# Layer 2 of a two-layer graph attention kernel reads the one-hot matrices that layer 1 stored; own lookups by quarters of a node tile; unnormalised weights with three more product columns

## Chip, cores and metric

The kernel runs on one core of one Trainium2 chip. The metric is the device time of one launch in microseconds (us), here the median of three runs. All times below are in us unless marked ns.

## The reference, cut to what matters

There are 3125 nodes with 768 features and 53125 edges sorted by their destination (50000 drawn ones and one loop per node). Each layer is a graph attention: it multiplies the features by a weight matrix, gives each edge a logit from its source and its destination, turns the logits into weights by a softmax over each destination's edges, and adds up the weighted source rows. A second loop per node is added inside, so a node's own row counts twice. Layer 1 has 4 heads of 256 columns, layer 2 one head of 768.

```python
def gat_conv(x, edge_index, W, a_src, a_dst, bias, heads, out_ch, concat):
    ei = _add_self_loops(edge_index, n); src, dst = (ei[0], ei[1])
    xl = (x @ W).reshape(n, heads, out_ch)
    e = leaky_relu(alpha_src[src] + alpha_dst[dst], 0.2)   # alpha: xl with a_src, a_dst
    m = segment_max(e, dst); e = exp(e - m[dst])
    alpha = e / (segment_sum(e, dst)[dst] + 1e-16)
    return segment_sum(xl[src] * alpha, dst) + bias
h = relu(layer_norm(x))
h1 = relu(layer_norm(gat_conv(h, W1...))) + (h @ Wr1 + br1)
h2 = layer_norm(gat_conv(h1, W2...)) + (h1 @ Wr2 + br2)
return x + h2
```

## The kernel before, in words

The nodes are cut into `NB` = 25 tiles of 128 (the last has 53). The edges of a node tile, without the loops, are laid into `S` = 2176 slots, which are `J` = 17 slot tiles of 128. Since the edges are sorted by destination, slot tile j holds only destinations of one or two of the node tile's four quarters of 32 nodes; the list `QUARTERS` (line 31) says which. For each slot three lists lie in HBM: the destination within the node tile (`rel16_d`), the source (`src16_d`) and the source modulo 128 (`slo16_d`). A flag computed on the chip sends inputs that do not fit to another function (`any_order`), which does not run here.

**Lookups.** The kernel has to bring logit parts to each slot: that of the slot's source (one of 3125 nodes) and those of its destination. It does this with products on TensorE. `spread` (line 444) loads a list of a node tile broadcast to all 128 partitions, `one_hot` (449) compares it with the partition number, which gives a 128 x 2176 matrix in bf16 with one 1 per slot. `own_products` (457) multiplies each of its 17 column blocks with the destination tile's logit parts, each split into three bf16 terms (`parts_of`, 434). `source_values` (467) multiplies the one-hot of the source modulo 128 with the logit parts of all 25 source tiles and picks the right one with a second one-hot, `ohh` (built at 469), in the operations `pick` and a reduction. Layer 1 does the own lookups beside its dense products (`own_lookups`, 843) and the source lookups afterwards (the loop at 954). Layer 2 does both in `softmax` (568) and builds all the one-hots once more.

**Softmax.** `weights` (488) brings the slots' logits into rows (25 per head, one per node tile, 2176 long) by transposes, takes the segment maximum with two scans and a maximum, goes back by transposes, and forms the exponentials. It then does the same way there and back once more for the segment sums, takes the reciprocal (555) and scales the weights `al`. For layer 2 it also scales the loop's weight (`alo2`).

**Sums.** `sums` (600) goes over the node tiles. For each of the up to 17 slot tiles GpSimd issues an indirect DMA (677) that gathers 128 source rows of the table (3 KB each in layer 2) into one of 26 buffers `g`. VectorE makes `w` (645 in layer 2), a 128 x 32 or 128 x 64 matrix with the slot's weight in the column of its destination. TensorE multiplies `w` by the gathered rows (697), with the slot tiles in six `ROUNDS` that mix quarters. In layer 2 `last_of` (654) makes a second such matrix `wl`, which carries the loop's weight at the last slot of each destination, and a one-column product with ones (702) brings it to the node (`aw`, 628). `finish` adds the node's own row, and `end2` (1134) the bias, the norm, the residual and the store. After each round a step of the residual `h1 @ Wr2` runs on TensorE (`residual`, 1083; 8 steps of 4 matmul instructions a node tile and a bias product).

**What sets the order.** TensorE, VectorE and ScalarE run the sums in the order of the program text; in layer 2's lookups and softmax only TensorE does, and a list scheduler orders the rest. Each engine and each DMA queue (SyncE's for loads and most stores, GpSimd's for gathers) runs in its order. The residuals of the first `FIRST` = 9 node tiles are filled in between lookups and softmax steps (`fill`), the other 16 run in the sums. The gathers of layer 2 are released by `mark` (594), a copy that waits for the lookups of the second-last node tile, and each waits until the memory of its buffer is free.

Of the kernel before, what the change touches and what calls it, by code (L numbers as in the profile page):

```python
# [9 lines left out]
F32 = mybir.dt.float32  # L10
# [14 lines left out]
SLOPE = 0.2  # L25
# [7 lines left out]
CODE = 4096  # L33

# [27 lines left out]
def in_order(  # L62
# [55 lines left out]
    rel16_d = dram.tile([NB * S], I16, name="rel16_d")  # L118
# [3 lines left out]

    parts_d = dram.tile([2, C2], F32, name="parts_d")
# [22 lines left out]
    rell_s = const.tile([128, NB * J], F32, name="rell_s")  # L146
    alone = const.tile([128, NB], F32, name="alone")
    ones_c = const.tile([128, 1], F32, name="ones_c")
    nc.vector.memset(ones_c, 1.0)
# [70 lines left out]
    def edge_list(ep, pe):  # L220
# [11 lines left out]
        nc.sync.dma_start(pk_d[E:].rearrange("(p f) -> p f", p=128), pad)  # L232
        yield
# [46 lines left out]
    def windows(pe):  # L280

        W = L + P
        with tc.tile_pool(name="cw", bufs=1, side="right", reuse_waits="tile") as ep:
# [38 lines left out]
            for i, d in enumerate((rel16_d, src16_d, slo16_d)):  # L322
                nc.sync.dma_start(d.rearrange("(p f) -> p f", f=L), r16[:, i])

        with tc.tile_pool(name="wn", bufs=1, side="right", reuse_waits="tile") as ep:
            k16 = ep.tile([NB, S], I16, name="k16")
            nc.sync.dma_start(k16, rel16_d.rearrange("(b f) -> b f", f=S))
# [4 lines left out]
            for t, to in ((k16, rel_s), (s16, idx_s), (k16, rell_s)):  # L332
                tf = ep.tile([NB, S], F32, tag="tf", name="tf")
                if to is rell_s:
                    nc.vector.memset(tf[:, S - 1:], 0.0)
                    nc.vector.tensor_tensor(tf[:, :S - 1], k16[:, :S - 1], k16[:, 1:], OP.is_equal)
                    nc.vector.scalar_tensor_tensor(tf, tf, float(CODE), k16, op0=OP.mult, op1=OP.add)
                else:
                    nc.vector.tensor_copy(tf, t)
# [104 lines left out]
    def spread(pool, b, list_d, name, bufs=2):  # L444
        t = pool.tile([128, S], I16, name=name, bufs=bufs)
        nc.sync.dma_start(t, list_d[b * S:(b + 1) * S][None, :].to_broadcast([128, S]))
        return t

    def one_hot(pool, b, list_d, name, t=None):

        if t is None:
            t = spread(pool, b, list_d, name)
        oh = pool.tile([128, S], BF16, name="oh" + name, bufs=2)
        nc.vector.tensor_scalar(oh, t, node_f, None, op0=OP.is_equal)  # L454
        return oh

    def own_products(heads, pp, oh, tabd_b):

        pd = pp.tile([128, J, 3, 2 * heads], F32, name="pd", bufs=1)
        for j in range(J):  # L460
            nc.tensor.matmul(pd[:, j], oh[:P, j * 128:(j + 1) * 128], tabd_b, start=True, stop=True)  # L461
        return pd

    def own_values(own, b, pd):
        nc.vector.tensor_reduce(own[:, :, :, b], pd.rearrange("p j t v -> p j v t"), axis=AX.X, op=OP.add)

    def source_values(heads, al, b, pp, nq, G, oh, tabs, ohh, pick):

        nc.vector.tensor_tensor(
            ohh, iota_f[:, None, :NB].to_broadcast([128, J, NB]),  # L470
            hi_s[:, b * J:(b + 1) * J, None].to_broadcast([128, J, NB]), OP.is_equal)
# [16 lines left out]
    def weights(heads, own, al, alo_d, sr, rows, pp, nq, fill, steps):  # L488
# [69 lines left out]
        if heads == 1:  # L558
            nc.vector.tensor_mul(alo_d, eo, s)
            return  # L560
# [7 lines left out]
    def softmax(heads, asad, al, alo_d, pp, nq, fill, side, steps=(4, 10, 3, 13, 5)):  # L568


        V = 2 * heads
        with tc.tile_pool(name="so", bufs=1, side=side, reuse_waits="tile") as so:
            own = so.tile([128, J, V, NB], F32, name="own")
            with tc.tile_pool(name="sb", bufs=2, side=side, reuse_waits="tile") as sb:

                part = parts_of(sb, asad.rearrange("p b v -> p (b v)"), NB * V, "part")
# [6 lines left out]
                for b in range(NB):  # L583
# [6 lines left out]
                    for _ in range((steps[0] + b % 2) // 2 if b > 1 else 0):  # L590
                        next(fill, None)
# [1025 lines left out]
```

## Time and profile before

| | us |
|---|---|
| three runs | 2020.69, 2017.33, 2020.15; median 2020.15 |
| the profiled execution's own time | 2020.3 |
| its span, first to last instruction | 2018.6 |
| busy in the span: PE | 1885.2 (93%) |
| DVE | 1249.0 (62%) |
| POOL | 877.6 (43%) |
| ACT | 277.2 (14%) |

The engines are PE (TensorE's matmuls; PEld are its weight loads, which overlap them), DVE (VectorE), ACT (ScalarE), POOL (GpSimd) and SP (SyncE). A busy PE is not PE at its peak, since matmuls are pipelined and their ends are modelled. In rows of groups the columns are: line, engine, operation, out<-in with sizes, count, busy time, mean ns of one, then the idle time of the engine just before them and what ended it. In rows of a timeline: start, length, engine, line, operation, count, and in brackets the idle time before it. In the chain of waits, which is followed back from the last instruction: start, length, what. The names of tiles carry no buffer numbers. A matmul in float32 shows as two instructions.

### The profile page before, as it was taken

The numbers are of one execution on the slowest core, as the hardware profiler recorded it, in microseconds if no ns is written. First come the engines' busy times: TensorE is split into PE (matmuls) and PEld (weight loads), VectorE is DVE, ScalarE is ACT, GpSimd is POOL, SyncE is SP. The second block draws the span as 40 slices with busy tenths as digits, with TensorE's granted clock in tenths as the row PEclk, the third lists the DMA queues.
The fourth block names the chain that finished last, engine by engine and source line by source line (L and its number), as shares of the span: only waits on it lengthen the run. The fifth ranks groups of instructions, "written<-read, shape, count | busy, mean of one in ns | idle before, by whom it ended". The sixth has DMA issues, their size and how long they took to land.

```text
span 2018.6 us, 38267 instructions
## 1 busy us (share of the span) xinstructions
PE 1885.2 (93%) x15033; PEld 1021.5 (51%) x15033; DVE 1249.0 (62%) x3352; ACT 277.2 (14%) x611; POOL 877.6 (43%) x911
## 2 busy tenths in 40 slices
PE   6999998999969999999999999789999999898986
PEld 4666665665424444544455554467544344343432
DVE  7774346888843555555456665468856655665665
ACT  1221463001201111112111111100100000000000
POOL 2200000000056656665666664000077777777774
PEclk9999999999989999999999999889999999998998
DMA  5531564331399999999999998588399999999996
GB/s 197 171 103 69 197 240 173 121 124 61 131 355 417 404 369 396 403 387 375 395 392 409 411 399 320 173 313 306 121 350 369 376 363 379 358 362 350 350 339 244
DMA packets 177687, 593.93 MB, mean 294 GB/s; under 512 B 32973, under 2 KB 45936, under 8 KB 177116
## 3 DMA queue, kind: packets, MB, share of 16 engines
q0 software_dynamic: 95840, 385.22, 50.0%
q1 hardware_dynamic: 78130, 196.57, 27.1%
q10 hardware_dynamic: 3530, 9.60, 1.2%
q8 instruction: 122, 2.00, 0.4%
q14 instruction: 65, 0.53, 0.1%
HBM read 528.32 MB, written 62.99 MB: 293 GB/s over the span
## 4 chain that ended last, share of the span: by engine, by line
PE 70%; DMA 14%; DVE 9%; POOL 3%; issue 2%; ACT 1%; SPq 0%; POOLq 0%; DVEq 0%; ACTq 0%
PE pa L697 18%; PE p L1052 13%; PE pm L800 13%; DMA g<-table,idx_s 11%; PE pr L1090 7%; PE pm L934 7%; PE pr L1002 4%; PE pq L478 4%; POOL g L677 3%; PE p L1030 1%; DMA s<-slo_d 1%; PE pd L461 1%; ACT h1T L1035 1%; PE pt L777 1%; DVE w L645 1%
## 5 line engine op out<-in xcount | busy, mean ns | idle before, releaser
L677 POOL DMA_INDIRECT g<-table,idx_s x832 | 827.4, 994 | 848.2 <-ACT rt L722 439.6
L697 PE MATMUL pa<-g,w 128*32 128x256 f32 (+1 forms) x6744 | 610.6, 426 | 75.2 <-DMA g<-table,idx_s 47.8
L697 PEld LDWEIGHTS pa<-g,w 128*32 128x32 f32 x6744 | 229.1, 110 | 417.9 <-issue 158.9
L1090 PE MATMUL pr<-wr,h 128*128 128x384 f32 (+1 forms) x800 | 299.3, 511 | 4.2 <-DMA h<-h1T_d 4.2
L1052 PE MATMUL p<-w,h1T 128*128 128x384 f32 (+2 forms) x800 | 278.2, 495 | 2.2 <-DVE h1T L1037 1.5
L800 PE MATMUL pm<-w,h 128*128 128x344 f32 (+1 forms) x900 | 271.9, 458 | 2.6 <-ACT h L779 2.6
L800 PEld LDWEIGHTS pm<-w,h 128*128 128x128 f32 (+1 forms) x900 | 166.7, 189 | 87.3 <-issue 6.9
L1052 PEld LDWEIGHTS p<-w,h1T 128*128 128x128 f32 (+1 forms) x800 | 143.8, 187 | 121.4 <-issue 34.1
L1090 PEld LDWEIGHTS pr<-wr,h 128*128 128x128 f32 (+1 forms) x800 | 142.2, 191 | 81.2 <-issue 13.8
L934 PE MATMUL pm<-h,wr 128*128 128x512 f32 x384 | 174.9, 607 | 0.0
L650 DVE TENSOR_TENSOR w<-oh,al 128x128 f32<-128x128 f32 (+1 forms) x416 | 141.6, 340 | 32.5 <-PE pa L697 12.3
L645 DVE TENSOR_SCALAR w<-iota_f,rel_s,al 128x32 f32<-128x32 f32 (+1 forms) x416 | 132.4, 325 | 44.7 <-PE pa L702 43.0
L659 DVE TENSOR_SCALAR wl<-iota_f,rell_s,alo 128x32 f32<-128x32 f32 (+1 forms) x416 | 134.9, 326 | 7.2 <-PE pa L702 6.7
L427 ACT ACTIVATE bn_sd<-bn_mv,eps 128x1 f32<-128x1 f32 (+1 forms) x50 | 14.7, 294 | 775.9 <-DVE bn_mv L423 729.7
L478 PEld LDWEIGHTS <-ohs 128*128 128x128 bf16 x2550 | 95.5, 97 | 35.8 <-issue 19.3
L934 PEld LDWEIGHTS pm<-h,wr 128*128 128x128 f32 x384 | 72.0, 194 | 79.5 <-issue 79.1
L1037 DVE TENSOR_TENSOR h1T<-h1T,r1t 128x512 f32<-128x512 f32 (+1 forms) x50 | 34.0, 680 | 125.9 <-ACT h1T L1035 120.6
L478 PE MATMUL pq<-tabs,ohs 128*128 128x100 bf16 (+1 forms) x2550 | 98.2, 191 | 11.3 <-DVE ohs L454 8.0
L649 DVE TENSOR_SCALAR oh<-iota_f,rel_s 128x32 f32<-128x32 f32 (+1 forms) x416 | 105.0, 252 | 4.8 <-DMA alo_d<-own 4.8
L1002 PE MATMUL pr<-h0k,wr 128*128 128x512 f32 (+1 forms) x288 | 106.8, 490 | 0.0
L1059 DVE COPY asad<-p 128x2 f32<-128x2 f32 (+1 forms) x25 | 4.0, 158 | 157.7 <-ACT row L1057 157.7
L702 PEld LDWEIGHTS pa<-ones_c,wl 128*32 128x32 f32 x1124 | 55.5, 112 | 56.9 <-issue 50.2
(222 smaller groups left out, 1493.0 us busy)
## 6 DMA issues: line engine op xcount, KB each, us to landing
d<-rel_d SPq DMA_DIRECT2D x50, 544.0 KB
s<-slo_d SPq DMA_DIRECT2D x50, 544.0 KB
g<-table,idx_s POOLq DMA_INDIRECT x832
table<-row SPq DMA_DIRECT2D x24, 512.0 KB
r1T_d<-rt SPq DMA_DIRECT2D x96, 128.0 KB
own<-table SPq DMA_DIRECT2D x24, 512.0 KB
r1t<-r1T_d SPq DMA_DIRECT2D x24, 512.0 KB
h1T_d<-h1T SPq DMA_DIRECT2D x24, 512.0 KB
```

The costliest lines, as they stand in the source:

```text
L478: nc.tensor.matmul(q[:, j], oh[:P, (j0 + j) * 128:(j0 + j + 1) * 128], tabs[:, i], start=(i == 0), stop=(i == 2))
L645: nc.vector.tensor_scalar(w[:, 0, :], iota_f[:, lo:hi], rel_s[:, c:c + 1], al[:, j, 0, b:b + 1], op0=OP.is_equal, op1=OP.mult)
L649: nc.vector.tensor_scalar(oh, iota_f[:, lo:hi], rel_s[:, c:c + 1], None, op0=OP.is_equal)
L650: nc.vector.tensor_tensor(w, oh[:, None, :].to_broadcast([128, heads, hi - lo]), al[:, j, :, b:b + 1].to_broadcast([128, heads, hi - lo]), ...
L659: nc.vector.tensor_scalar(w, iota_f[:, lo:hi], rell_s[:, c:c + 1], alo_d[:, j, 0, b:b + 1], op0=OP.is_equal, op1=OP.mult)
L677: nc.gpsimd.indirect_dma_start(out=g, out_offset=None, in_=table[:, :], in_offset=bass.IndirectOffsetOnAxis(ap=idx_s[:, b * J + j:b * J + ...
L697: nc.tensor.matmul(pa[32 * q:32 * q + 32, o // f, o % f:o % f + n], w[:, o // cols, :], g[:, o:o + n], start=to not in opened, stop=False, ...
L800: nc.tensor.matmul(pm[:r, :C], h0[gi][:, k, o:o + r], w1[:, k, i * C:(i + 1) * C], start=(k == 0), stop=(k == NK1 - 1))
L934: nc.tensor.matmul(pm[:, :GB * P], wr1[:, k, m * 128:(m + 1) * 128], h0[gi][:, k, :], start=(k == 0), stop=(k == NK1 - 1))
L1002: nc.tensor.matmul(pm[:, :nb], wr1[:, k, m * 128:(m + 1) * 128], loaded[gi, k][:, :nb], start=(k == 0), stop=(k == NK1 - 1))
L1052: nc.tensor.matmul(pm[:, :n], hT[:, k, :r], w2[:, k, o:o + n], start=(k == 0), stop=(k == NK2 - 1))
L1090: nc.tensor.matmul(pm[:, :384], h1[:, k, :r], wr2[:, k, i * 384:(i + 1) * 384], start=(k == 0), stop=False)
```

## The change

1. Layer 1 stores each node tile's one-hot matrices in HBM (`hot_d`, 128 x 3369 bf16 a node tile): the own one, the source one, and `ohh`, which is now bf16. The stores are issued on GpSimd's queue. Layer 2 loads them with one DMA a node tile into four buffers and builds none; `softmax` is gone.
2. Own lookups by quarters: partition group q (32 nodes) only sees slots 512q - 128 to 512q + 640 (`WIN` = 768, read from `rel16_d` with 128 entries in front). The one-hot has 768 columns instead of 2176; the table is spread over four column groups, of which each node fills its own quarter's (`by_quarter`); 6 products of 4 x 6 x heads columns take the place of 17 of 6 x heads.
3. Layer 2's weights stay unnormalised: `shares` does only the maximum's half of the softmax. Each `w` is multiplied with three columns `ends2` (1, whether the slot holds the maximum's weight or more, and that times twice the loop's weight), so the sum of the weights and the loop's weight come out in three PSUM columns beside the sums. `finish` makes the loop's weight `aw` and the factor `share` from them with six small operations, and `end2` scales. `wl`, `last_of`, `rell_s` and `alone` are gone.
4. `FIRST` is 3 instead of 9, and layer 2's residual steps run one a node tile from node tile 10 on in the lookups; the loads of `wr2` are spread over the lookups. With it there are 7 instead of 13 `xr` buffers.

```diff
+WIN = 768
+    hot_d = dram.tile([NB, 128, S + WIN + J * NB], BF16, name="hot_d")
...
-            for t, to in ((k16, rel_s), (s16, idx_s), (k16, rell_s)):
+            for t, to in ((k16, rel_s), (s16, idx_s)):
...
+    def window(pool, b):
+        t = pool.tile([128, WIN], I16, name="near", bufs=3)
+        for q in range(4):
+            o = b * S + 512 * q
+            nc.sync.dma_start(t[32 * q:32 * q + 32], rel16_d[o:o + WIN][None, :].to_broadcast([32, WIN]))
+        return t
+    def by_quarter(t, v, n, heads):
+        for i in range(3):
+            nc.vector.tensor_tensor(t[:, :, :, i, :], v(i)[:, :, None, :].to_broadcast([P, n, 4, 2 * heads]),
+                                    mine[:, None, :, None].to_broadcast([P, n, 4, 2 * heads]), OP.mult)
+    def own_products(heads, pp, oh, tabd_b, bufs=1):
+        pd = pp.tile([128, 512], F32, name="pd", bufs=bufs)[:, :20 * 6 * heads]
+        at = pd.rearrange("p (g r v) -> p r g v", r=4, v=6 * heads)
+        for c in range(WIN // 128):
+            nc.tensor.matmul(at[:, c % 4, c // 4:c // 4 + 4], oh[:, c * 128:(c + 1) * 128],
+                             tabd_b.rearrange("p q t v -> p (q t v)"), start=(c == 0), stop=True,
+                             skip_group_check=True)
...
+    def shares(al, own, share, ends, sr, pp, fill, steps):
...
+        nc.vector.tensor_tensor_scan(fw, pen[:, 0:S], xs, 0.0, op0=OP.add, op1=OP.max)
+        nc.vector.tensor_tensor_scan(bw[:, ::-1], pen[:, 1:S + 1][:, ::-1], xs[:, ::-1], 0.0, op0=OP.add, op1=OP.max)
+        nc.vector.tensor_max(fw, fw, bw)
...
+        nc.vector.tensor_sub(al, al, m)
+        nc.scalar.activation(share, al, AF.Exp)
+        nc.vector.tensor_sub(eo, eo, m)
+        nc.scalar.activation(eo, eo, AF.Exp)
+        nc.vector.tensor_scalar(ends[:, :, :, 1], al, -1.0, None, op0=OP.is_ge)
+        nc.vector.scalar_tensor_tensor(ends[:, :, :, 2], eo, 2.0, ends[:, :, :, 1], op0=OP.mult, op1=OP.mult)
...
             if heads == 1:
-                nc.vector.tensor_max(aw[:r], pa[:r, 1, f:f + 1], alone[:r, b:b + 1])
+                at = pa[:r, 1, f:f + 3]
+                v = gp.tile([P, 4], F32, name="v", bufs=2)[:r]
+                nc.vector.tensor_scalar(v[:, 0:1], at[:, 1:2], 0.1, 2.0, op0=OP.is_lt, op1=OP.mult)
+                nc.vector.tensor_scalar(v[:, 1:2], at[:, 1:2], 0.1, None, op0=OP.max)
+                nc.vector.reciprocal(v[:, 1:2], v[:, 1:2])
+                nc.vector.scalar_tensor_tensor(v[:, 2:3], at[:, 2:3], v[:, 1:2], v[:, 0:1], op0=OP.mult, op1=OP.add)
+                nc.vector.tensor_scalar(v[:, 3:4], at[:, 0:1], v[:, 2:3], 1e-16, op0=OP.add, op1=OP.add)
+                nc.vector.reciprocal(v[:, 3:4], v[:, 3:4])
+                aw, share = v[:, 2:3], v[:, 3:4]
...
-                        wl = last_of(b, j) if heads == 1 else None
...
-                    for q, wl in ends:
-                        nc.tensor.matmul(pa[32 * q:32 * q + 32, 1, f:f + 1], wl, ones_c, start=False, stop=False,
+                    for q, w, v in ends:
+                        nc.tensor.matmul(pa[32 * q:32 * q + 32, 1, f:f + 3], w, v, start=False, stop=False,
...
-                                ohs[b] = one_hot(sb, b, rel16_d, "d", ds_.pop(b))
+                                ohs[b] = one_hot(sb, ds_.pop(b), WIN, "ohd")
+                                nc.gpsimd.dma_start(hot_d[b, :, S:S + WIN], ohs[b])
...
+                        ohs = one_hot(sb, t, S, "ohs")
+                        nc.gpsimd.dma_start(hot_d[b, :, :S], ohs)
+                        ohh = sb.tile([128, J, NB], BF16, name="ohh", bufs=3)
...
+                        nc.gpsimd.dma_start(hot_d[b, :, S + WIN:], ohh.rearrange("p j b -> p (j b)"))
+                        source_values(H, al1, b, pp, 4, group_of(H), ohs, tabs, ohh, pick)
...
-        FIRST = 9
+        FIRST = 3
...
+                    for b in range(NB):
+                        hot = sb.tile([128, S + WIN + J * NB], BF16, name="hot", bufs=4)
+                        nc.sync.dma_start(hot, hot_d[b])
+                        pick = sb.tile([128, J, 1, NB], F32, name="pick")
+                        source_values(1, al, b, pp, 3, J, hot, tabs,
+                                      hot[:, S + WIN:].rearrange("p (j b) -> p j b", b=NB), pick)
+                        own_values(own, b, own_products(1, pp, hot[:, S:S + WIN], tabd[:, b]))
+                        if 1 <= b <= NK2:
+                            nc.sync.dma_start(wr2[:, b - 1, :], Wr2[(b - 1) * 128:b * 128, :])
+                        if b == 5:
+                            load(0)
+                        if b > NK2 + 1:
+                            next(fill)
+                        if b == NB - 2:
+                            behind = nc.gpsimd.tensor_copy(mark, al[:, 0, 0, b:b + 1]).ins
+                with tc.tile_pool(name="sr2", bufs=1, side="right", reuse_waits="tile") as sr:
+                    shares(al[:, :, 0, :], own, al2[:, :, 0, :], ends2, sr, pp, fill, (8, 4))
...
-            def end2(b, z):
-                nc.vector.tensor_add(z, z, b2_b[:z.shape[0]])
+            def end2(b, z, share):
+                nc.vector.scalar_tensor_tensor(z, z, share, b2_b[:z.shape[0]], op0=OP.mult, op1=OP.add)
```

More of the change, by code (lines that the diff above doesn't have):

```diff
@@ L232, in edge_list @@
         nc.sync.dma_start(pk_d[E:].rearrange("(p f) -> p f", p=128), pad)
+        none = ep.tile([1, P], I16, name="none")
+        nc.vector.memset(none, P)
+        nc.sync.dma_start(rel16_d[:P], none)
         yield
@@ L636, in finish @@
                                                pa[:r, o // f, o % f:o % f + n], op0=OP.mult, op1=OP.add)
-            yield from end(b, z)
+            yield from end(b, z, share)
         def weights_of(b, j):
@@ L1143, in in_order @@
             with tc.issue_after(behind):
-                sums(1, C2, table2, al2, alo2, 26, 1, gp, pp, end2, more, [each] * len(ROUNDS))
+                sums(1, C2, table2, al2, ends2, 26, 1, gp, pp, end2, more, [each] * len(ROUNDS))
 @with_exitstack
```

171 lines of the change are left out of this document (80 added, 91 removed).

## The prediction

> **What bounds the kernel now.** I read three views in this order: the page's span, the busy time by stage, and the timeline of GpSimd (POOL) in the second layer. The stages are layer 1's source lookups (350 to 485 us), layer 2's lookups (1288 to 1420), its softmax (1420 to 1461) and its sums (1461 to the end). Columns: stretch, busy time of PE, weight loads, DVE, ACT and POOL with instruction counts, granted clock, DMA share, GB/s.
>
> ```profile
> span 2018.6 us, 38267 instructions
> ```
>
> ```profile
> core 0: us, PE busy (x) PEld busy (x) DVE busy (x) ACT busy (x) POOL busy (x), PEclk, DMA share, GB/s
> 350.00:485.00 135.00, 133.15 (x1313) 85.98 (x1311) 114.61 (x151) 11.00 (x16) 0.00 (x0) 1.00 0.32 108
> 1288.00:1420.00 132.00, 116.56 (x1905) 81.24 (x1904) 92.61 (x220) 0.97 (x2) 1.65 (x2) 0.92 0.86 304
> 1420.00:1461.00 41.00, 38.74 (x168) 23.46 (x167) 34.82 (x28) 7.94 (x14) 0.00 (x0) 1.00 0.24 80
> 1461.00:2019.00 558.00, 494.26 (x3950) 222.15 (x3948) 342.97 (x1122) 7.36 (x25) 411.62 (x415) 0.97 0.95 349
> ```
>
> In the sums PE looks like the bound (494 of 558 us) and DMA too (0.95). The timeline of POOL says otherwise:
>
> ```profile
> 1414.45 0.67 POOL L594 COPY mark<-al 128x1 f32<-128x1 f32 x1 [171.53 <-DMA xr<-in_x_dram]
> 1415.50 0.98 POOL L677 DMA_INDIRECT g<-table,idx_s  x1 [0.38 <-DMA xr<-in_x_dram]
> 1461.29 1.16 POOL L677 DMA_INDIRECT g<-table,idx_s  x1 [44.81 <-DVE s L551]
> 1462.75 0.95 POOL L677 DMA_INDIRECT g<-table,idx_s  x1 [0.30 <-issue]
> ...
> 1999.64 0.95 POOL L677 DMA_INDIRECT g<-table,idx_s  x1 [0.30 <-issue]
> ...
> 2013.11 0.95 ACTq L172 DMA_DIRECT2D out_dram<-z  x2
> ```
>
> The first gather goes out at 1415.5; the second waits 44.8 us for DVE, because its buffer lies on memory that the softmax still uses (line 551). From 1461.3 to 2000.6 the other 415 gathers follow without a break, one every 1.300 us (539.3 / 415), and 18.0 us after the last one the span ends. The groups of the sums confirm it:
>
> ```profile
> L677 POOL DMA_INDIRECT g<-table,idx_s x393 | 390.2, 993 | 121.3 <-issue 75.9 <-DMA g<-table,idx_s 23.8 <-PE pa L702 13.7
> L697 PE MATMUL pa<-g,w 128*32 128x384 f32 x2168 | 281.5, 503 | 50.9 <-DMA g<-table,idx_s 35.0 <-DVE w L645 6.0 <-DVE wl L659 5.4
> L1090 PE MATMUL pr<-wr,h 128*128 128x384 f32 x457 | 174.8, 512 | 0.0
> L659 DVE TENSOR_SCALAR wl<-iota_f,rell_s,alo 128x32 f32<-128x32 f32 x250 | 79.0, 317 | 6.8 <-PE pa L702 6.3 <-PE pa L697 0.5
> L702 PE MATMUL pa<-ones_c,wl 128*32 128x1 f32 x1084 | 46.2, 170 | 0.0
> ```
>
> POOL's idle time is 121.3 / 393 = 0.31 us ahead of each gather, the constant gap between two issues: it never waits for a buffer, while PE waits for gathers (35.0 us) and DVE. So the end is **the start of the gather run, plus 539 us, plus 18 us**, and an edit pays if it moves that start, or the layer 1 before it.
>
> **The change, part by part.**
>
> *Layer 2's lookups.* The timeline has the end of their last reduction, the chain of waits their start (1298.9, when the last node tile's logits exist; that stays) and one tile:
>
> ```profile
> 1418.18 0.59 DVE L483 TENSOR_REDUCE al<-pick 128x17 f32<-128x425 f32 x1
> ```
>
> ```profile
> 1298.92 0.20 DVE part L438
> ...
> 1346.16 1.27 PE pq L478 x51
> 1347.44 0.42 PE pd L461 x17
> 1347.86 2.69 PE pr L1090 x8
> ```
>
> Now a tile costs PE 1.27 + 0.42 + 2.69 = 4.38 us, the last being two residual steps. After, the 17 own products become 6 (6 x 0.025 = 0.15), there is no residual step up to tile 9, and one (1.34) from tile 10: 1.42, then 2.76 us a tile. DVE loses both one-hots and `ohh`:
>
> ```profile
> L454 DVE TENSOR_SCALAR ohs<-s,node_f 128x2176 bf16<-128x2176 int16 x25 | 19.5, 779 | 10.2 <-DMA s<-slo_d 10.2
> L469 DVE TENSOR_TENSOR ohh<-iota_f,hi_s 128x425 f32<-128x425 f32 x25 | 14.8, 595 | 0.5 <-PE p L1030 0.5
> ```
>
> Of its 92.6 us in this stage 2 x 19.5 + 14.8 go; the 39 left bound nothing. What bounds it is DMA. A tile now loads 128 x 3369 x 2 B = 0.862 MB instead of two broadcasts of 0.557 MB. In the changed program four of these loads stand ahead of the last `table2` store on SP's queue, the rest behind it, so they flow from 1299: 21 x 0.862 + `wr2` 3.15 + four `h1` 2.10 + four `xr` 1.57 = 24.9 MB. At what rate?
>
> ```profile
> DMA packets 12175, 40.08 MB, mean 304 GB/s; under 512 B 2296, under 2 KB 2296, under 8 KB 12157
> ```
>
> ```profile
> 1500.00:1550.00 50.00, 44.79 (x352) 19.98 (x348) 32.09 (x112) 0.59 (x2) 38.42 (x39) 1.00 1.00 382
> ```
>
> The stage before, with its waits, had 304; a full stretch of gathers 382. Rows of 6.7 KB that stand queued are nearer to the second; I take 370: 67 us, to 1366. PE's own bound is close: tile 10 lands after 10.1 MB, at 1326, and 15 x 2.76 us later it is 1368. With the last picks and reductions the lookups end at **1372**, instead of at 1418.8. Bounds: 1368 (PE) and 1385 (304 GB/s). SP's new waits (for a free `hot` buffer, and one `h1` load that waits for a residual on PE with five `hot` loads behind it) have three loads in flight to cover them.
>
> The Trainium skill, DMA: Bandwidth & Descriptors, section Specifications, gives 358 GB/s as HBM's limit for a core; by it the lookups would end 2 us later. The row with 382 disagrees.
>
> *Start of the gathers.* The gather buffers now lie lower (fewer `xr` and no `wl` buffers): only the second and third touch softmax memory, the tile `keep`, whose last reader is the instruction that makes `pen`. In the changed program this stands on DVE behind the last reduction and four small operations, and ahead of the scans. So the run starts at 1372 + 4 = **1376**, 85 us earlier. But now it runs beside the scans:
>
> ```profile
> 1424.05 4.68 DVE rows L530
> 1428.72 4.59 DVE bw L531
> 1433.34 2.41 DVE rows L533
> ```
>
> ```profile
> 1715.04 0.95 POOL L677 DMA_INDIRECT g<-table,idx_s  x1 [0.31 <-PE pa L702]
> ...
> 1716.22 0.96 DVE L1135 TENSOR_TENSOR z<-z,b_b 128x768 f32<-128x768 f32 x1
> 1716.29 1.71 POOL L677 DMA_INDIRECT g<-table,idx_s  x1 [0.30 <-issue]
> ```
>
> A gather issued just after DVE began an operation on two SBUF tensors took 1.71 instead of 0.95 us: it ended about when it could if it had waited for DVE's end. Scans and maximum (11.7 us) are such operations, and some five of 0.6 us besides. If one gather slips through at each boundary, the run loses some **8 us**; bounds 0 and 14.7. The gain is 85 - 8 = 77 us.
>
> The Trainium skill, SBUF — State Buffer, section Who interferes with whom, has it that DVE with two SBUF inputs and GpSimd share a port under an exclusive lock, held for a whole instruction. The two rows agree; taken strictly it is the 14.7 us, 7 more than my sum, and it speaks against this overlap.
>
> *The softmax* loses its second pass of scans, sums, transposes and the reciprocal; it is not what the gathers wait for any more. Weights `w` exist some 26 us after 1372 (transposes, the scans and maximum above, exponentials, two residual additions): at about 1399. With 26 buffers and a gather each 1.3 us POOL doesn't run out by then (23 / 1.3 = 18).
>
> *The sums.* `wl` goes (391 operations of DVE, by the row of its narrower form 317 ns each), six small operations a node tile come; DVE had slack. The three-column products take the place of the one-column ones, as many. The cost is in `FIRST` = 3: six more residuals, 22 instead of 16, run here. A round of PE when nothing is late:
>
> ```profile
> 1834.48 1.56 PE L1090 MATMUL pr<-wr,h 128*128 128x384 f32 x4
> 1835.97 1.50 PE L697 MATMUL pa<-g,w 128*32 128x384 f32 x16
> 1837.28 0.22 PE L702 MATMUL pa<-ones_c,wl 128*32 128x1 f32 x8
> 1837.43 1.56 PE L1090 MATMUL pr<-wr,h 128*128 128x384 f32 x4
> ```
>
> One residual step takes 1.49 us, the round's products 1.46. After, 176 steps fall on 141 rounds: 1.46 + 1.25 x 1.49 + 0.09 for the biases = 3.41 us for 2.77 gathers, 1.23 us a gather against POOL's 1.30. From 1399 PE needs 415 x 1.23 = 510 us, to 1909; the last gather is issued at 1376 + 8 + 539 = 1923. PE stays hidden, with some 14 us to spare. DMA carries 5.5 MB more, about 10 GB/s, on top of the 349, below the 382 seen. The last tile's end gains five small operations: **+1 us**.
>
> *Layer 1.* Its PE is full, so PE's work counts:
>
> ```profile
> 300.74 0.41 PE pd L461 x17
> ...
> 337.88 2.30 PE pq L478 x51
> ```
>
> ```profile
> L343 PE MATMUL pe<-ident,tf x51: 214/215/238, 148.1 to 185.0; 25*128 25x25 f32 x51
> ```
>
> Six own products of 96 columns instead of 17 of 24: by the 100-column ones (2.30 / 51 = 0.045) 0.27 us instead of 0.41, 25 times: 3.5 us. A third of the list's transposes go, 17, about 1.3 us. The 75 stores of 21.6 MB go through POOL's queue, empty there, beside DMA at 108 GB/s over 135 us; the one-hots have a third buffer. They may delay DVE (114.6 busy of 135) a little. Windows of the lists cost SP 75 more issues but fewer bytes. I take **-5 us**, bounds -8 and 0.
>
> **Sum:** -77 + 1 - 5 = -81. The profiled execution took 2020.3 us (span 2018.6), the median is 2020.15, so nothing is added between them: 2020.3 - 81 = **1939 us**. With the bounds (lookups -4 to +13, lock -8 to +7, layer 1 -3 to +5) its own range is 1924 to 1964.
>
> **Rivals.**
>
> *PE becomes the bound of the sums and the moved residuals come back.* For it: busy times, 281.5 + 46.2 us for 393 gathers and 174.8 us for 457 instructions, so 346 for 415 gathers and 22 x 32 x 0.383 = 269 with no overlap, some 615 us. From 1399 it ends at 2014, plus the 18 and 1 us of the end, less 5 and plus 1.7 around the span: 2030, **slower**. It decides from (1923 - 1399) / 415 = 1.26 us of PE a gather on, and costs more than the change brings from (2018.6 + 5 - 19 - 1399) / 415 = 1.46. Against: the round above, which shows the products overlapping the steps at 1.23. Between lies 1.30 to 1.42 (throttled clock, products that come singly because gathers do): 1955 to 2004.
>
> *The gathers don't start early*: the memory or the lock holds them until `w` exists, at 1399, as the softmax holds them now. Then 1399 + 539 + 19 - 5 + 1.7 = 1954. Against: only `keep` overlaps.
>
> *The change doesn't shorten the lookups*: loads of 6.7 KB rows wait on each other and the stage ends at 1418 as now. Then 46 us are lost: 1985. Against: the 382 row.
>
> **How the numbers follow.** Forecast 0.70; gathers held 0.08; PE a partial bound 0.10; lookups as slow as now 0.05; PE adding up, slower, 0.05; below 1922 (issue nearer its 1.25 us) 0.02. The range 1922 to 1985 takes in the forecast, the held gathers and half of the partial bound, 0.83. All but the slower case and a sliver of the partial ones are faster: faster 0.93, within 0.2% 0.02, slower 0.05 (0.2% is about what a measurement of this kernel tells from none).
>
> **What would show it.** Lookups ending near 1367 in the new trace (layer 1's 5 us off); a second gather some 4 us later, POOL gathers of 2 to 5 us beside the scans; then 1.30 us each with 0.30 of idle time; PE waiting for gathers in the sums. It is wrong if POOL waits there for `pa` products (PE bound), if `hot` loads land more than 3 us apart, or if layer 1's lookups slow under the stores.

## The result, and the profile after

Four runs of the changed kernel gave a median of 1939.9 us (1936.9 to 1944.2), four of the kernel before 2020.4: a ratio of 0.9603 with a 95% interval of 0.9576 to 0.9629. The forecast was 1939. The profiled execution took 1944.2 us, the slowest of the four; its span is

```profile
span 1942.4 us, 36923 instructions
```

76.2 us shorter than that of before. Where these 76.2 us came from is read from four points in time. The timeline of VectorE in the changed kernel has two of them, the start of layer 2's lookups (`part`) and the last reduction of a lookup (`al`), and the scans:

```profile
1286.08 0.19 DVE L440 CAST part<-asad 128x50 bf16<-128x50 f32 x1
...
1366.27 0.59 DVE L492 TENSOR_REDUCE al<-pick 128x17 f32<-128x425 f32 x1
...
1371.04 4.68 DVE L601 TENSOR_TENSOR_SCAN fw<-pen,xs 25x2176 f32<-25x2176 bf16 x1
1376.56 4.67 DVE L602 TENSOR_TENSOR_SCAN bw<-pen,xs 25x2176 f32<-25x2176 bf16 x1
1381.27 2.41 DVE L603 TENSOR_TENSOR fw<-fw,bw 25x2176 f32<-25x2176 f32 x1
```

The timeline of GpSimd has the others, the start of the gather run and its last gather:

```profile
1364.12 0.18 POOL L1167 COPY mark<-al 128x1 f32<-128x1 f32 x1 [133.26 <-DMA xr<-in_x_dram]
1365.41 0.97 POOL L699 DMA_INDIRECT g<-table,idx_s  x1 [1.11 <-DMA keep<-keep_d]
1371.71 4.78 POOL L699 DMA_INDIRECT g<-table,idx_s  x1 [5.32 <-PE pr L1119]
1376.80 5.20 POOL L699 DMA_INDIRECT g<-table,idx_s  x1 [0.30 <-issue]
1382.30 2.21 POOL L699 DMA_INDIRECT g<-table,idx_s  x1 [0.31 <-issue]
1384.81 0.95 POOL L699 DMA_INDIRECT g<-table,idx_s  x1 [0.30 <-issue]
...
1921.58 0.95 POOL L699 DMA_INDIRECT g<-table,idx_s  x1 [0.30 <-issue]
```

| stretch | before | after | difference | forecast |
|---|---|---|---|---|
| start to the lookups of layer 2 | 1298.9 | 1286.1 | -12.8 | -5 |
| the lookups | 119.9 | 80.8 | -39.1 | -47 |
| end of lookups to second gather | 42.5 | 4.9 | -37.6 | -38 |
| second to last gather, with its issue | 539.3 | 550.8 | +11.5 | +8 |
| last gather to the end | 18.0 | 19.9 | +1.9 | +1 |

That the total came out at the forecast is luck in one respect: two terms, layer 1 and the lookups, were off by the same 8 us in opposite directions. The three gathers beside the two scans and the maximum took 4.78, 5.20 and 2.21 instead of 0.95 us, which is 9.3 us. Each ended some 0.8 us after the VectorE operation beside it (the scan from 1371.04 ended at 1375.72, the gather at 1376.49).

**Where layer 1 gained 13 us.** The timeline of TensorE ahead of layer 1's source lookups, first in the kernel before (own products `pd`, residual products `pm`, the first source lookups `pq`):

```profile
319.86 0.57 PE L461 MATMUL pd<-tabd,ohd 128*128 128x24 bf16 x17 [0.68 <-DVE own L465]
322.17 0.60 PE L461 MATMUL pd<-tabd,ohd 128*128 128x24 bf16 x17 [1.73 <-DVE own L465]
325.59 0.61 PE L461 MATMUL pd<-tabd,ohd 128*128 128x24 bf16 x17 [2.82 <-DVE own L465]
326.04 5.19 PE L934 MATMUL pm<-h,wr 128*128 128x512 f32 x8
331.07 1.11 PE L478 MATMUL pq<-tabs,ohs 128*128 128x100 bf16 x21
```

and then in the changed one:

```profile
313.02 0.42 PE L471 MATMUL pd<-tabd,ohd 128*128 128x96 bf16 x6
314.11 0.41 PE L471 MATMUL pd<-tabd,ohd 128*128 128x96 bf16 x6 [0.68 <-DVE own L477]
314.36 3.67 PE L956 MATMUL pm<-h,wr 128*128 128x512 f32 x8
317.86 2.46 PE L487 MATMUL pq<-tabs,ohs 128*128 128x100 bf16 x51
```

The source lookups begin 13.2 us sooner, and from there to layer 2 nothing more is won or lost (12.8): the 75 stores cost nothing that can be seen. (The run without stores below, `e6_build`, says the same: its layer 2 began at 1306.3, those of two runs with stores on the same chip, `e7_no_steps` and `e8_lean`, at 1305.9 and 1303.9.) Before, the last own lookups stood in a row behind the dense products, each waiting for VectorE; now fewer are left over and their waits are short.

**The lookups of layer 2** have two halves. Busy time by stretch in the changed kernel (stretch, length, busy PE, weight loads, DVE, ACT and POOL with counts, granted clock, DMA share, GB/s):

```profile
1287.00:1327.00 40.00, 25.50 (x693) 21.49 (x693) 16.15 (x41) 0.00 (x0) 0.00 (x0) 0.50 0.99 387
1327.00:1367.00 40.00, 37.52 (x793) 28.66 (x792) 17.60 (x42) 0.00 (x0) 1.16 (x2) 0.94 0.82 296
```

and the chain of waits where one half goes over into the other:

```profile
1310.69 11.99 DMA hot<-hot_d
...
1322.73 1.54 PE pq L487 x51
1324.27 0.16 PE pd L471 x6
1324.43 2.75 PE pr L1119 x4
1327.18 1.34 PE pq L487 x51
1328.53 0.15 PE pd L471 x6
1328.68 1.39 PE pr L1119 x4
...
1344.15 0.32 SPq L1107
...
1344.58 6.87 DMA hot<-hot_d
...
1351.49 1.49 PE pq L487 x51
...
1353.14 2.70 PE pr L1119 x4
```

Until 1322.7, when tile 11 has landed, the chain goes mostly through the loads, with DMA full at 387 GB/s; then it goes through TensorE, at 2.8 us a tile, of which 1.39 are a residual step. Once more, at tile 20, it goes through a load: the queue had stood until 1344.15 at the load of an `h1` (line 1107), which had to wait for a residual, and TensorE then waited 2.48 us for the one-hots behind it. The steps after both waits took 2.75 and 2.70 us instead of 1.39.

### The profile page after: what moved, and what is told of

Read it like the earlier page. It is cut to its first block, busy times and chain, and to the rows that moved or that the text cites. A ratio compares the mean times of both kernels' runs of the same rounds, so it can differ in the third digit from the quotient of the medians.

```text
span 1942.4 us, 36923 instructions
## 1 busy us (share of the span) xinstructions
PE 1830.3 (94%) x14432; PEld 995.0 (51%) x14432; DVE 1093.4 (56%) x2923; ACT 246.1 (13%) x606; POOL 930.0 (48%) x986
## 5 line engine op out<-in xcount | busy, mean ns | idle before, releaser
L699 POOL DMA_INDIRECT g<-table,idx_s x832 | 839.8, 1009 | 436.4 <-issue 158.8
L718 PE MATMUL pa<-g,w 128*32 128x256 f32 (+1 forms) x6744 | 572.5, 422 | 50.0 <-DMA g<-table,idx_s 28.7
L718 PEld LDWEIGHTS pa<-g,w 128*32 128x32 f32 x6744 | 220.8, 110 | 367.1 <-issue 172.9
L676 DVE TENSOR_SCALAR w<-iota_f,rel_s,al 128x32 f32<-128x32 f32 (+1 forms) x416 | 99.2, 327 | 54.6 <-PE pa L723 49.8
L429 ACT ACTIVATE bn_sd<-bn_mv,eps 128x1 f32<-128x1 f32 (+1 forms) x50 | 14.7, 295 | 753.4 <-DVE bn_mv L425 709.5
L889 POOL DMA_DIRECT2D hot_d<-ohd x25 | 13.5, 542 | 199.8 <-DVE own L440 114.5
L1063 ACT ACTIVATE h1T<-p,be_c,g_c 128x128 f32<-128x128 f32 (+1 forms) x200 | 74.7, 457 | 68.4 <-PE p L1058 67.4
L723 PEld LDWEIGHTS pa<-ends,w 128*32 128x32 f32 x1124 | 49.0, 111 | 56.1 <-issue 53.6
L652 DVE TENSOR_SCALAR v<-pa 128x1 f32<-128x1 f32 (+1 forms) x25 | 4.0, 159 | 130.2 <-PE pa L723 130.2
```

The costliest lines, as they stand in the source:

```text
L676: nc.vector.tensor_scalar(w[:, 0, :], iota_f[:, lo:hi], rel_s[:, c:c + 1], al[:, j, 0, b:b + 1], op0=OP.is_equal, op1=OP.mult)
L699: nc.gpsimd.indirect_dma_start(out=g, out_offset=None, in_=table[:, :], in_offset=bass.IndirectOffsetOnAxis(ap=idx_s[:, b * J + j:b * J + ...
L718: nc.tensor.matmul(pa[32 * q:32 * q + 32, o // f, o % f:o % f + n], w[:, o // cols, :], g[:, o:o + n], start=to not in opened, stop=False, ...
L723: nc.tensor.matmul(pa[32 * q:32 * q + 32, 1, f:f + 3], w, v, start=False, stop=False, skip_group_check=True)
L1063: nc.scalar.activation(hT[:, k0 + k, :r], pt[:, k, :r], AF.Relu, bias=be1_c[:, k0 + k:k0 + k + 1], scale=g1_c[:, k0 + k:k0 + k + 1])
```

## Experiments

Ratios are to the kernel before on the same chip; a difference from the changed kernel is that of the ratios, times the time before. The first four ran on a chip on which the kernel before took 2022, so they stand beside the 0.9603 above. The next four ran on another chip, on which it took 2136, the last four on a third, 2132. On the third the changed kernel was run again (`a0_after`, 0.9721), and the runs of the second chip are set beside that. Two kernels ran on both; their ratios differ by 0.0019 (e7, 4 us) and 0.0004 (e8, 1 us) between the chips, and a difference across them is no surer than that.

**Gathers after the scans.** `mark` is written from the result of the maximum instead of the second-last tile's logits:

```diff
-                            behind = nc.gpsimd.tensor_copy(mark, al[:, 0, 0, b:b + 1]).ins
...
         nc.vector.tensor_max(fw, fw, bw)
+        behind = nc.gpsimd.tensor_copy(mark[:NB], fw[:, 0:1]).ins
```

> The changed kernel, but its gathers start only when the scans and their maximum are over. Theory (the end is the start of the gather run plus its issues plus a tail of 20 us, and scans that overlap gathers hold POOL up by 9 us): the run starts at 1383.7 instead of 1371.7, but no gather is held, so 12.0 - 9.3 = 2.7 us later than the changed kernel, about 1942.6; gathers of 0.95 us from the start. Rival 1 (the slow gathers beside the scans have another cause, such as a queue that fills): they are slow at the start of any run, and it ends 12 us later, 1952. Rival 2 (PE sets the end, from the time when the weights exist): no difference.

Measured: 1948.0, ratio 0.9633 (0.9620 to 0.9646), 6 us later, though the intervals of the two ratios overlap. The timeline of its GpSimd:

```profile
1385.41 0.18 POOL L604 COPY mark<-fw 25x1 f32<-25x1 f32 x1 [152.62 <-DVE fw L603]
1386.70 0.97 POOL L701 DMA_INDIRECT g<-table,idx_s  x1 [1.12 <-issue]
1387.98 0.95 POOL L701 DMA_INDIRECT g<-table,idx_s  x1 [0.30 <-issue]
```

No gather is held by a scan any more, so it was the scans that held them, and rival 1 falls. The expectation forgot that 1.3 us pass from `mark` to the first gather, and that one gather was out already; with these 2.6 us the theory gives 5.3. The profiled executions show less: from the end of the lookups to the start of the last gather this one took 555.5 us, the changed kernel 554.7, since 415 gathers here came at 1.295 us each and 411 there, behind the held ones, at 1.306. So whether the overlap with the scans pays, by a few us or not at all, is not settled.

**Gathers after the weights.** The same with `mark` written from the last of `ends` (line 620), so that the run waits for the whole softmax.

> The changed kernel, but its gathers start only when the last of the weights exist (some 1394). Theory (end = start of the gathers plus issues plus tail): the run starts at 1394 without held gathers; the changed kernel's started at 1371.7 and lost 9.3 to the scans, which is as if at 1381.0: 13 us later, 1953. Rival (PE sets the end from the weights on): PE's first product comes 2 to 3 us later, and so does the end, 1943.

Measured: 1957.7, 0.9684 (0.9669 to 0.9699), 16 us later. Its first and its last gather:

```profile
1395.17 0.98 POOL L700 DMA_INDIRECT g<-table,idx_s  x1 [1.11 <-DMA h<-h1T_d]
...
1933.67 1.52 POOL L700 DMA_INDIRECT g<-table,idx_s  x1 [0.30 <-issue]
```

The span ended at 1954.3, 20.6 us behind the last issue's start; in the changed kernel it was 20.8. Between the two profiled executions the last issue moved by 12.1 us, where the theory has 13 and its rival 2 to 3: the end moved with the start of the gathers, as the theory has it. It is also the price of the second rival of the forecast (1954), which did not happen.

**One tile for `keep` and `pen`.**

```diff
-        pen = sr.tile([NB, S + 2], BF16, name="pen")
+        pen = keep
```

> The changed kernel, but pen is made in place of keep, so that the softmax needs 4.4 KB less a partition and no gather buffer lies on it. Theory: the second gather follows the first one, at about 1366.7 instead of 1371.7, loses about 1 us more to four two-input operations of DVE, and the end comes 4 us sooner, 1936. Rival (PE sets the end): no difference, 1940. Rival 2 (something else than keep holds the second gather): no difference, and the second gather still at 1371.

Measured: 1938.5, 0.9583 (0.9570 to 0.9596). That is 4 us sooner, though the intervals of the two ratios overlap; from the end of the lookups to the last issue it is 551.6 against 554.7 us. Its gathers:

```profile
1367.19 0.98 POOL L699 DMA_INDIRECT g<-table,idx_s  x1 [1.11 <-issue]
1368.47 0.96 POOL L699 DMA_INDIRECT g<-table,idx_s  x1 [0.31 <-issue]
```

The second one follows the first at once, in place of 6.3 us later, and rival 2 falls: it was the memory that held it. The row of the changed kernel names a residual step (`PE pr`) as what ended that wait, but the same steps run here too. Where no step runs there (`e7_no_steps`, below), the row names `pen`, the last reader of `keep`:

```profile
1379.90 4.78 POOL L699 DMA_INDIRECT g<-table,idx_s  x1 [5.79 <-DVE pen L588]
```

**More work for TensorE in the sums.**

```diff
             for k in range(NK2):
+                for k_ in ((0, k) if k < 3 and b >= FIRST and k else (k,)):
```

> The changed kernel with two more residual steps of PE in each of the 22 residuals of the sums (the first chunk's products are added twice more, so these residuals aren't the reference's): 44 x 1.39 = 61 us of PE work, without a load, a gather or an operation of DVE more. Theory (PE hidden behind POOL with 14 us to spare, as the prediction counted): 47 us later, 1987. By the idle time that PE shows in the sums of the changed kernel (540 - 505 = 35 us): 26 us later, 1966. Rival (PE already sets the end): 61 us later, 2001.

Measured: 1944.4, 0.9614 (0.9600 to 0.9629), 2 us later and within the interval of the changed kernel. All three numbers were too high. Groups of TensorE in the sums (1395 to 1938), first of the changed kernel:

```profile
L1119 PE MATMUL pr<-wr,h 128*128 128x384 f32 (+1 forms) x704 | 258.1, 504 | 0.0
L718 PE MATMUL pa<-g,w 128*32 128x384 f32 x2247 | 252.4, 494 | 24.0 <-DMA g<-table,idx_s 13.6 <-DVE w L676 8.1 <-DVE bn_mv L425 1.3
L1123 PE MATMUL pr<-ball_r,ones_r 2*128 2x384 f32 (+1 forms) x44 | 13.4, 383 | 0.0
```

then of this one, with a stretch of its sums (start and end, length, busy PE):

```profile
L1120 PE MATMUL pr<-wr,h 128*128 128x384 f32 (+1 forms) x880 | 313.5, 499 | 0.0
L718 PE MATMUL pa<-g,w 128*32 128x384 f32 x2246 | 221.1, 491 | 1.3 <-DMA g<-table,idx_s 1.1 <-DVE w L676 0.2
```

```profile
1400.00:1900.00 500.00, 500.00 (x3981) 246.08 (x3983) 243.84 (x753) 6.48 (x22) 381.52 (x383) 1.00 0.99 373
```

55 us more of residual steps, and 31 us less of the same products: products that come singly, each behind its gather, count longer than 16 in a row, as two rows of the changed kernel show (0.21 against 0.09 us each):

```profile
1502.10 1.50 PE L718 MATMUL pa<-g,w 128*32 128x384 f32 x16
...
1509.00 0.84 PE L718 MATMUL pa<-g,w 128*32 128x384 f32 x4 [0.82 <-DMA g<-table,idx_s]
```

So the busy time of a waiting TensorE is not its work. Its work in the changed kernel, estimated from 1.46 us for 16 products and 1.39 for a step, is 2247 / 16 x 1.46 + 176 x 1.39 + 13 = 463 us; from 1394 that ends at 1857, 65 us ahead of the last gather. With 61 more TensorE is busy all through this window (478.7 of 500 us in the changed kernel), and the end has at most just begun to move: the last gather started 0.3 us later.

**The own lookups of layer 1 later.** Four empty steps stand where the third list of slots had its four:

```diff
+            for _ in range(4):
+                yield
             hi_i = ep.tile([128, NB * J], I32, name="hi_i")
```

> The changed kernel with four empty steps in place of the four that the third list took in the work beside layer 1's products: layer 1's own lookups begin about 17 us later again, as before (229.8 and not 212.7). Theory (own lookups that are left over behind the last product, one after the other through DVE, are 8 of the 13 us that layer 1 gained): the source lookups start at about 325 instead of 317.9, and the end comes 7 to 8 us later, about 1948. Rival (the 13 us are PE's shorter products and transposes alone): 0 to 1 us later, 1940.

Measured: 2086.6, 0.9767 (0.9745 to 0.9788), against 0.9721 (0.9700 to 0.9742) of the changed kernel on the third chip: 10 us later. Its TensorE:

```profile
327.81 0.64 PE L473 MATMUL pd<-tabd,ohd 128*128 128x96 bf16 x6 [1.95 <-DVE own L479]
328.25 5.29 PE L958 MATMUL pm<-h,wr 128*128 128x512 f32 x8
333.37 2.46 PE L489 MATMUL pq<-tabs,ohs 128*128 128x100 bf16 x51
```

The row of late own lookups is back, and most of what layer 1 gained is gone. On the same chip `e7_no_steps`, whose layer 1 is that of the changed kernel, began its source lookups at 318.9 and layer 2 at 1305.9; here it is 333.4 and 1317.1. The profiled execution of this kernel also has 5.3 us of waits for the residual's weights (1.30, 3.63 and 0.34, from 310 to 320 us), which the theory did not have; so how much of the 10 us belongs to the one and to the other is only bounded: 5 to 10.

**No stored matrices.** Layer 2 loads the lists and makes its one-hots, layer 1 stores none; all else stays:

```diff
-                        nc.gpsimd.dma_start(hot_d[b, :, :S], ohs)
...
-                        nc.sync.dma_start(hot, hot_d[b])
+                        near = window(sb, b)
+                        t = sb.tile([128, S], I16, name="s", bufs=2)
+                        nc.sync.dma_start(t, slo16_d[b * S:(b + 1) * S][None, :].to_broadcast([128, S]))
+                        ohs = one_hot(sb, t, S, "ohs", 2)
+                        ohd = one_hot(sb, near, WIN, "ohd", 2)
```

> The changed kernel without stored one-hot matrices: layer 2 makes them itself from the lists (own lookups by quarters, three residuals and unnormalised weights stay); layer 1 stores nothing. Theory (the lookups were shortened by the residual steps that left them and by the quarters; stored matrices only relieve DVE): a tile costs DVE 0.78 + 0.42 + 0.60 + 0.60 + 0.26 + 0.59 = 3.25 us, 25 tiles 81 us, as long as the 81 us of the changed kernel: 0 to 4 us later, 1940 to 1944. Rival (the stored matrices carry the gain of the lookups): they take some 110 us, 29 us later, 1969.

Measured: 2100.7, 0.9825 (0.9798 to 0.9852), 22 us later. The lookups took 104.3 us (1306.3 to 1410.6), against 81.1 in the changed kernel on the third chip and 80.8 on the first. Its TensorE:

```profile
1341.10 1.54 PE L487 MATMUL pq<-tabs,ohs 128*128 128x25 bf16 x51 [2.74 <-DVE ohs L457]
...
1345.54 1.54 PE L487 MATMUL pq<-tabs,ohs 128*128 128x25 bf16 x51 [2.74 <-DVE ohs L457]
```

The theory's 81 falls. A tile takes 4.44 us (4.02 from tile 12 on) though neither engine is full: VectorE makes the next tile's `ohs` only behind this tile's `pick`, which waits for TensorE, which waits for `ohs`. So about 23 of the 39 us that the lookups became shorter hang on the stored matrices. By the trace that is not because they spare VectorE work but because they take it out of this circle: VectorE is busy for 2.8 us a tile, and waits for loads only 1.5 us in the whole stage. No run made the one-hots ahead of `pick`, so this reason is read from the trace and not shown by a run.

**No residual steps beside the lookups** (`FIRST` = 1, seven `xr` buffers as in the changed kernel):

```diff
-        FIRST = 3
+        FIRST = 1
...
-                        if b > NK2 + 1:
-                            next(fill)
```

> The changed kernel with one residual ahead of the sums instead of three, and none of its steps beside the lookups; 24 residuals run in the sums. Theory (lookups bounded by DMA in their first half and by PE's residual steps in their second; PE has about 60 us to spare in the sums): 24 MB at 395 GB/s, so the lookups end at about 1350 instead of 1366.9, the gathers start 17 us sooner, and so does the end: 1923. Rival 1 (PE has the 14 us to spare that the prediction counted): 24 us of steps more cost 10, 1933. Rival 2 (the loads bound the lookups all along): no difference, 1940.

Measured: 2065.3, 0.9656 (0.9631 to 0.9680), 14 us sooner than the changed kernel's 0.9721 on the third chip.

**The same, lean.** `pen = keep`, and the loads of `wr2` moved from among the one-hot loads into `early`, which starts with the first residual step, behind the load of `keep`:

```diff
-                        if 1 <= b <= NK2:
-                            nc.sync.dma_start(wr2[:, b - 1, :], Wr2[(b - 1) * 128:b * 128, :])
...
-                    shares(al[:, :, 0, :], own, al2[:, :, 0, :], ends2, sr, pp, fill, (8, 4))
+                    shares(al[:, :, 0, :], own, al2[:, :, 0, :], ends2, sr, pp, fill, (4, 6))
```

> As e7, and pen is made in place of keep, and the weights of the residual are loaded behind the one-hot matrices and keep, no longer among them; the four steps ahead of the scans' transposes and six behind. Theory: 18.1 MB at 395 GB/s end the lookups at about 1335, 32 us sooner, the second gather needs no wait (5 us), the run still loses 9 to the scans: 35 us sooner than the changed kernel, 1905. Rival 1 (PE, which starts the sums at some 1368, sets the end): 0.495 us of products a gather, 192 + 1.39 us of steps at most: 1368 + 205 + 270 + 20 = 1863, so it doesn't. Rival 2 (weights come later behind the residual's loads, and POOL runs out of its 26 buffers): 1910 to 1920.

Measured: 2056.0, 0.9618 (0.9598 to 0.9638). That is 22 us sooner than the changed kernel on the third chip, for 35 forecast; on a chip this slow in the sums the 1905 could not come out. The lookups took 60.9 us instead of the 46 expected (18.1 MB at 395 GB/s). Its SyncE queue issued the 21 loads in this time:

```profile
1307.86 46.13 SPq L1162 DMA_DIRECT2D hot<-hot_d  x21
```

The issuing took 46 us, as the loads at 395 GB/s should, but it began 4 us behind the lookups' start, when the first of four buffers came free, and the last tile's products began 8 us after it.

**Beside the changed kernel.** On the third chip ran the changed kernel, e7 and e8 once more, and e9, which is e8 with `ohh` made by VectorE:

```diff
-                        nc.gpsimd.dma_start(hot_d[b, :, S + WIN:], ohh.rearrange("p j b -> p (j b)"))
...
+                        nc.vector.tensor_tensor(
+                            ohh, iota_f[:, None, :NB].to_broadcast([128, J, NB]),
+                            hi_s[:, b * J:(b + 1) * J, None].to_broadcast([128, J, NB]), OP.is_equal)
```

> The changed kernel itself, so that e7, e8 and e9 are compared with it on one chip. On a chip like that of the first comparison: 1940, 0.960 of the time before. On one like that of the last four runs (time before 2136, POOL held in the sums by gathers that land late): by e1, less the 12 us by which e1's layer 1 ended later than e7's and e8's there, 2087 - 12 = 2075, 0.972.

> e7 once more, beside the changed kernel. Theory (the lookups were held by PE's residual steps, and PE has the room for them in the sums): 17 us sooner than the changed kernel where POOL is never held in the sums (1923); where gathers land late, 10 us sooner, as e1 and e7 showed. Rival (no room on PE): 7 us sooner at most, or none.

> e8 once more, beside the changed kernel. Its lookups took 60 us in the last run, with DMA idle for the first 5 us until the first buffer came free and pauses of 2 to 4 us. Theory: 81 - 60 = 21 us from the lookups and 5 from pen, 26 us sooner than the changed kernel where POOL is never held in the sums (1914), 19 where gathers land late. Rival (weights come too late, POOL runs out of buffers): 10 to 15 us sooner.

> e8, but the tile one-hot (ohh, 425 of 3369 columns) is neither stored nor loaded: DVE makes it, 0.60 us a tile. Theory (DMA bounds the lookups of e8): 2.3 MB less, 6 us sooner than e8. Rival (DVE's order: making the next tile's one-hot waits behind this tile's pick, as the making of all three did in e6): PE waits for nothing of DVE's, so no loss, but where loads aren't the bound nothing is won either: the same as e8.

| | median | ratio (95%) | lookups |
|---|---|---|---|
| changed kernel | 2071.2 | 0.9721 (0.9700 to 0.9742) | 81.1 |
| e7 | 2055.6 | 0.9637 (0.9616 to 0.9658) | 68.6 |
| e8 | 2050.6 | 0.9614 (0.9595 to 0.9632) | 64.3 |
| e9 | 2044.3 | 0.9611 (0.9581 to 0.9641) | 60.4 |

The changed kernel came out as expected. All three others beat both kernels: e7 by 18 us over the changed one (10 expected on such a chip, 17 on one like the first), e8 by 23 (19 and 26), e9 by 23. The 24 us of residual steps that they put into the sums cost nothing that can be seen. e9's lookups are 4 us shorter than e8's, but its time is not told apart from e8's. What they would take on a chip like the first was not tried.

## Why the prediction was right, point by point

**What bounds the kernel: right on the first chip.** The end is the start of the gather run, some 540 us of issues and 20 us of tail. e2, e3 and e4 moved only the start: e3 moved the last issue by 12.1 us and e4 by -3.1, counted from the end of the lookups, and the end followed; e2's 0.8 is too small to tell. It is a statement about such chips, though. GpSimd's gathers in the sums, first in the changed kernel of the result above (1400 to 1940), then in `a0_after` (1400 to 2032):

```profile
L699 POOL DMA_INDIRECT g<-table,idx_s x400 | 400.0, 1000 | 122.6 <-issue 72.0 <-DMA g<-table,idx_s 29.0 <-PE pa L723 12.1
```

```profile
L699 POOL DMA_INDIRECT g<-table,idx_s x412 | 408.6, 992 | 224.7 <-issue 91.4 <-remote 70.6 <-PE pa L723 42.7
```

The busy time is the same, but the idle time is 0.55 instead of 0.31 us a gather: there GpSimd waits 42.7 us for the products that free its buffers and 70.6 us for something that the trace only calls remote, and the run took 646 us instead of 551.

**Layer 2's lookups: direction right, size 8 us off.** 370 GB/s was too low a rate for the loads (387) and still the estimate was too early. Tile 10 came 30 us after the start, not 27. Behind it loads of `h1` and `xr` held tile 11 back by another 4 us, and tile 20 came 2.5 us too late behind the `h1` load that waits for a residual. So the step that failed here is "three loads in flight to cover them": they did not cover it. After each of the two waits a residual step took 1.4 us longer (2.75 and 2.70 instead of 1.39, granted clock 0.50 and 0.59). Against that, the 4 us set aside for the last picks were not needed: 3 + 4 + 2.5 + 2.8 - 4 is some 8. That two bounds follow one another, DMA and then the residual steps, was in the forecast; e7 shows the second by taking it away. The sign that was to show the forecast wrong, one-hot loads that land more than 3 us apart, did appear (by the starts of TensorE's products, six of the seven gaps from tile 4 to tile 11, 3.05 to 6.6 us). It was badly set: the forecast's own 27 us for seven tiles are 3.9 us each. The 358 GB/s of the Trainium skill (DMA: Bandwidth & Descriptors, section Specifications), which the prediction quotes, did not bind here, where DMA moved 387.

**Start of the gathers: right.** 4.9 us for the 4, held by `keep`, as e4 and the row of e7 show.

**The lock: right, 9.3 us for 8.** By the Trainium skill, SBUF — State Buffer, section Who interferes with whom, the side that comes second is blocked for the whole instruction of the first. The trace agrees: each held gather ended with VectorE's operation plus some 0.8 us. The 14.7 us of the strict bound did not come: by the rows, one gather got out at each boundary. The whole run of gathers grew by 11.5 us; the remaining 2.2 were not traced.

**The sums: right that TensorE is hidden, wrong by how much.** "510 us, 14 us to spare" was the step that failed. It took 1.49 us for a residual step where 1.39 is right when steps come in pairs (a row of eight instructions in the changed kernel is followed 2.78 us later by the next products), and its 2.77 gathers a round don't fit its 141 rounds (they make 390 gathers, not 415). The work is 463 us, and e5 shows some 60 to spare. So the slower rival was given its price, some 615 us, from busy times that count waiting as work; at 463 us, 1.12 a gather, it was further away than the forecast had it.

**Layer 1: 13 instead of 5 us.** The terms (shorter products, fewer transposes) were counted as TensorE's work alone. What was missed is order: the third list also held four steps of the work beside the products, so own lookups now begin 17 us sooner (212.7 against 229.8) and fewer are left over for the end. e1 puts the four steps back and loses 10 us, of which 5 to 10 belong to this order.

The rivals: TensorE (PE) as the bound is ruled out by e5; gathers held until the weights exist would have cost what e3 did; lookups that are no shorter did not occur, and e6 shows what they would have needed: one-hots still made by VectorE.

## What to carry to other kernels

Where issues of a queue set the pace, follow back what releases the first of them: a single tile's memory can decide when a 540 us run begins. A busy engine that waits between its instructions looks full; price its spare time from a stretch in which it runs without a wait, or give it more work and see whether the end moves. And count an edit to work that is stepped beside other work in steps too: what begins sooner leaves less for the end.

## What the runs showed of the hardware

- One kernel took 1940 us on one chip and 2071 on another; on both it was faster than the kernel before, but not held by the same things in the sums. Rates of DMA in the sums of `a0_after`, 1 us a column from 1600 on:

```profile
GB/s 418 421 412 422 387 387 406 393 399 221 111 276 184 227 12 0 104 283 166 276 344 301 164 160 212 323 430 397 424 426 422 416 406 387 393 387 399 406 338 55
```

  DMA reaches rates as in the changed kernel of the result above, where the same 40 us had 293 to 437, but drops to 0 and 12 between them. Why stays open. The Trainium skill, HBM Reference, section Specifications (TRN2), has it that two cores share a memory domain and that one alone can reach 425 GB/s; no run here shows whether another core was at work.
- TensorE had a granted clock of 0.50 for the whole 40 us in which it waited a little for most tiles' loads (busy 25.5 of 40), and 0.94 over the next 40, in which it mostly ran through. One wait of 2.48 us, ahead of tile 20, was enough to lower it: 1.00 from 1340 to 1349, and 0.59 over the 4.1 us behind the wait. By the Trainium skill, TensorE: Matmul & The Clock Gate, section What's actually happening, the clock is half or full, and full only after some 3.4 us of sustained work. The row of the first 40 us agrees as to the half clock, with gaps of 0.7 to 3.6 us; but a stretch of 5.7 us in it without a gap (from 1287.83) stayed at 0.50 as well, so 3.4 us of work are not enough wherever they fall.
